# Starting layer 2's masked weights inside layer 1's last group, with a shrinking lead

## The chip, the cores and the metric

The kernel runs on one core of one Trainium2 chip. The metric is the device time of one execution in microseconds (us). The engines are TensorE (PE, matrix products), VectorE (DVE, elementwise), ScalarE (ACT, activations), GpSimd (POOL) and SyncE (SP, which issues most DMAs). Each engine works its own queue in order and waits on semaphores for the others.

## The reference, cut to what matters

Four layers of graph attention work on x (16 batches, 1024 nodes, 64 channels, float32) and one adjacency matrix adj (1024 x 1024). After each, x becomes layernorm(x + layer(x)). Layer 1 and layer 2 are the ones around the change:

```python
# layer 1: softmax over the neighbours, for each channel by itself
feat = softplus(x * (INV_SQRT2 * w0) + b0)
scores = feat * wa + ba
attn = softmax(where(mask, scores, -1e9), over neighbours)      # mask = adj > 0
out = einsum('bijd,bjd->bid', attn, feat)

# layer 2 (layer 0 is of the same form)
h = input @ W
e = (h @ a1)[:, :, None] + (h @ a2)[:, None, :]
e = where(e > 0, e, 0.2 * e)
attention = softmax(where(adj > 0, e, -9e15))
out = elu(attention @ h)
```

Layer 3 has four heads of dot-product attention and an output layer of the same kind.

## The kernel before, in words

The 1024 nodes are 8 chunks (C) of 128, and the 16 batches (B) are 4 groups (NG) of 4 (GB) in layer 1.

**Layer 1** is a sum over neighbours of numerator and denominator, each split in a high and a low part (`hi`, `lo`). `product_l1(g, ic)` is 16 products on PE for chunk `ic` of group `g` (L1966). `average(g, ic)` takes the logarithm and the exponential on ACT (L1976, L1977), four passes on DVE (L1979 to L1984) and four `bn_stats` (L1986). Results lie in a PSUM pool with two buffers. Between the chunks stand hand-placed tasks: `ahead` (preparations for the next group, in the last group those of layer 2) and `last` (the previous group's or layer's endings: `root`, `shift` and eight `rows` tasks, which scale eight rows each on ACT, L780). A scheduler orders the engines' queues here.

**Layer 2** is `gat_layer` with `zero_mean`. Its engines' queues keep the written order. For batch b and chunk k:

- `unit(k)` on DVE (L1026) makes the masked weights of 128 x 1024, e = max(G, q) * aT. G is the exponential of the scores for a pair of batches, q a factor per node, aT the mask. The `e` tiles have 7 buffers in this layer.
- `product(k, e)` on PE (L1038) multiplies them with `vals`, four matmul instructions of 64 x 512 in the trace (two calls).
- The loop `go()` runs over t = 0 to 15 and k = 0 to 7. In each step it issues unit k, queues the product of the unit two steps before (LAG = 2), and then the tasks that `slots[(t, k)]` holds.
- The ends of a batch are among these: `evict` (ACT, L1057), `project` (PE, L1070), `divide` (DVE reciprocal and ACT `l_sums`, L1114), `quotients` (ACT L1124 and the exponential m, L1136), `residual` (DVE v and m, L1141, L1142), `norm` (DVE), `root`, `shift`, `store` (ACT, L780).
- So are the preparations for a pair of batches: `prep_x` (transposes, PE L933, ACT L934), `prep_s` (scores, PE L940), `prep_top` (DVE maximum L951, ACT copy `l_s` L952, POOL all-reduce L957), `prep_p` (four small ACT instructions, L965 to L974), `prep_G` for two halves (PE `pg` L987, ACT exponential into G, L996, from a PSUM pool with one buffer), and `prep_v` (ACT, nine small instructions into `vals`, L1006, L1008).

Before the change, batch 0's x, scores, top and p are in the last group of layer 1, and its G and vals are written after that group. The first unit follows layer 1's last average and moments. Layer 1's last four batches get their rows (`last`) within the first steps of layer 2.

```python
e = unit(k)
behind(lambda product=product, k=k, e=e: product(k, e), LAG if zero_mean else 2 * LAG)
```

Of the kernel before, what the change touches and what calls it, by code (L numbers as in the profile page):

```python
# [8 lines left out]
F32 = mybir.dt.float32  # L9
F32R = mybir.dt.float32r  # L10
# [6 lines left out]
P = 128  # L17
# [20 lines left out]
LAG = 2  # L38
# [544 lines left out]
def fast_path(  # L583
# [25 lines left out]
    B, N, D = x.shape  # L609
    C = N // P  # L610
# [4 lines left out]
    NG = B // GB  # L615
    HALF = N // 2
    CH = C // 2
# [4 lines left out]
    ep = ctx.enter_context(tc.tile_pool(name="ep", bufs=2))  # L622
# [6 lines left out]
    for g in range(NG):  # L629
        t = xpool.tile([P, C, GB, D], F32, tag=f"x{g}", name=f"x{g}")  # L630
# [161 lines left out]
    def behind(step, lag):  # L792
        waiting.append(step)
        while len(waiting) > lag:
            waiting.pop(0)()
# [6 lines left out]
    aT = const.tile([P, C, N], BF16, tag="aT", name="aT")  # L802
# [108 lines left out]
    def gat_layer(w, name, zero_mean, own, room=None):  # L911
# [3 lines left out]

        w1, w4, ind, s12, sums, w_out = (w[k] for k in ("w1", "w4", "ind", "s12", "sums", "out"))
        F = D - 1 if zero_mean else D
        xT, G, pgs, pq, vals, only, stats = {}, {}, {}, {}, {}, {}, {}
        if not zero_mean:
            ring = [gp.tile([P, C, 32], F32, tag=f"only{r}", name=f"only{r}", bufs=1) for r in range(4)]  # L920
            for t in ring:
# [65 lines left out]
                nc.tensor.matmul(parts[i], w1[rows, :], xT[b][h][rows, :], start=True, stop=True)  # L987

        def exps_G(b, h):
            if h == 0:  # L990
                G[b] = gp.tile([P, 2, N], F32, tag="G", name=f"G_{name}_{b}")
            cols = slice(h * HALF, (h + 1) * HALF)
            parts = pgs[b, h]
            for i, part in enumerate(parts):
                dst = G[b][:, :, cols] if len(parts) == 1 else G[b][:, i, cols]
                nc.scalar.activation(dst, part, AF.Exp, bias=pq[b][2], scale=1.0 - ALPHA)  # L996

        def prep_G(b, h):
            scores_G(b, h)
# [1 line left out]

        def prep_v(b):
            p = pq[b - b % 2][0][:, :, b % 2]
            v = gp.tile([P, C, D], F32, tag="vals", name=f"vals_{name}_{b}", bufs=3)
            for c in range(C):
                nc.scalar.activation(v[:, c, :F], xb(b)[:, c, :F], AF.Copy, scale=p[:, c : c + 1])  # L1006
            if zero_mean:
                nc.scalar.copy(v[:, :, F], p)  # L1008
            else:
                only[b] = ring[b % 4]  # L1010
                nc.scalar.copy(only[b][:, :, b % 2], p)
            vals[b] = v

        def attention(b):
# [7 lines left out]
            begins, closes = b % 2 == 0 or not joint, b % 2 == 1 or not joint  # L1022

            def unit(k):
                e = gp.tile([P, N], F32, tag="e", name="e", bufs=7 if zero_mean else 10)
                nc.vector.scalar_tensor_tensor(  # L1026
                    e, G[b - b % 2][:, b % 2, :], pq[b - b % 2][1][:, k, b % 2 : b % 2 + 1], aT[:, k, :],
                    ALU.max, ALU.mult,
                )
                return e  # L1030
# [149 lines left out]
        def at(t, k, task):  # L1180
            slots.setdefault((t, k), []).append(task)

        work = [attention(b) for b in range(B)]
        if zero_mean:
            ends = [(1, 1), (1, 3), (1, 4), (1, 5), (2, 0), (2, 1)]
# [7 lines left out]
        for b in range(B):  # L1193
            places = ends[b % 2]
# [11 lines left out]
        ahead = []  # L1206
        for b in range(0, B, 2):
            halves = (range(CH), range(CH, C)) if zero_mean else (range(C), ())
            chain = [
                lambda b=b: prep_x(b, 0), lambda b=b: prep_x(b, 1), *(lambda b=b, c=c: prep_s(b, c) for c in halves),  # L1210
                lambda b=b: prep_top(b), lambda b=b: prep_p(b), lambda b=b: prep_G(b, 0),
                lambda b=b: prep_G(b, 1), lambda b=b: prep_v(b), lambda b=b: prep_v(b + 1),
            ]
            if zero_mean:
                places = (-2, 0), (-2, 1), (-2, 5), (-2, 6), (-1, 0), (-1, 2), (-1, 3), (-1, 4), (-1, 2), (0, 4)
            else:
                places = (-3, 3), (-3, 3), (-3, 7), (-3, 7), (-2, 1), (-2, 3), (-2, 7), (-1, 3), (-1, 4), (0, 4)
            if b == 0 and not zero_mean:
                chain[6:8] = [lambda f=f, h=h: f(0, h) for f in (scores_G, exps_G) for h in range(2)]
                ahead = chain[:-1]  # L1220
                at(0, 4, chain[-1])
                continue
            if b == 2 and not zero_mean:
                places = (-2, 4), (-2, 5), (-2, 6), (-2, 6), (-2, 6), (-2, 7), (-1, 1), *places[7:]
            for task, (t, k) in zip(chain, places):
                if b + t >= 0:
                    at(b + t, k, task)
                elif b:
                    at(0, 0, task)
                else:  # L1230
                    ahead.append(task)
        if room:
            ahead[-3:-1] = [lambda f=f, h=h: f(0, h) for f in (scores_G, exps_G) for h in range(2)]

        def go(extra, opening=()):
            for (t, k), todo in extra.items():
                for task in todo:
                    at(t, k, task)
            with tc.manual_schedule(engines=in_order):
                for task in opening:  # L1240
                    task()
                for t in range(B + 1):
                    for k in range(C):
                        catch_up()
                        if t < B:
                            unit, product, _ = work[t]
                            e = unit(k)
                            behind(lambda product=product, k=k, e=e: product(k, e), LAG if zero_mean else 2 * LAG)
                        elif t == B and k == 0:
                            drain()  # L1250
                        if t < B or (t == B and k < own):
                            for task in slots.get((t, k), []):
                                task()

            return [
                task for t in range(B, B + 3) for k in range(C) for task in slots.get((t, k), []) if (t, k) >= (B, own)
            ]
# [567 lines left out]
    def prep_l1(g, q):  # L1825
# [36 lines left out]

        def back():
            if q == 0:
                his[g] = l1["halves"].tile([P, C, 2, 2, P], F32R, tag="hi", name=f"hi{g}")
                los[g] = l1["halves"].tile([P, C, 2, 2, P], F32R, tag="lo", name=f"lo{g}")
            t = h["t"]
            pe = l1["psum"]("pe")
            for c in range(C):
                nc.tensor.transpose(pe[:, c, :], t[:, c, :], ident)  # L1870
            hi, lo = his[g][:, :, q, 1, :], los[g][:, :, q, 1, :]
            nc.scalar.copy(hi, pe)
            nc.vector.tensor_tensor(h["f"], h["f"], pe, ALU.mult)
            nc.vector.tensor_tensor(lo, pe, hi.bitcast(F32), ALU.subtract)
# [11 lines left out]
    with tc.tile_pool(name="ps_g", bufs=1, space=bass.MemoryType.PSUM, reuse_waits="tile") as ps_g, tc.tile_pool(  # L1886
# [64 lines left out]
    l2_ahead, l2_go = gat_layer(later["w2"], "l2", True, 2, room=dict(  # L1951
        xT=lambda: [ep.tile([P, C, D], F32, tag="v", name="xT").rearrange("p c d -> p (c d)") for _ in range(2)],
        g=lambda: l1["psum"]("pg").rearrange("p (i c) q -> p i (c q)", i=2),
    ))
    l1_psum = ExitStack()
    ps_l = l1_psum.enter_context(tc.tile_pool(name="ps_l", bufs=2, space=bass.MemoryType.PSUM, reuse_waits="tile"))
    with tc.tile_pool(name="l1", bufs=2, reuse_waits="tile") as pool:
# [36 lines left out]
        for g in range(NG):  # L1994
            ahead = [[] for _ in range(C)]
            for q in range(2 if g + 1 < NG else 0):

                for ic, task in zip((q, q, q, q, q + 1, q + 2, q + 2, q + 4, q + 5), prep_l1(g + 1, q)):
                    ahead[ic].append(task)
            if g + 1 == NG:  # L2000
                for ic, task in zip((1, 2, 3, 3, 4, 5, 6, 6), l2_ahead):
                    ahead[ic].append(task)
            st = pool.tile([P, C * GB, 6], F32, tag="st1", name=f"st{g}")
            for ic in range(C):
                po = product_l1(g, ic)
                average(g, ic, po, st)
                for task in ahead[ic] + last[ic : ic + 1]:
                    task()
            y = xg[g].rearrange("p c b d -> p (c b) d")
            mo = {}  # L2010

            root, finish = moments(st)

            def shift(mo=mo, end=finish):
                mo["n"] = end()

            def rows(c, y=y, mo=mo):
                scaled(y, y, mo["n"], range(c * 8, c * 8 + 8))

            last = [root, shift] + [lambda c=c, rows=rows: rows(c) for c in range(C * GB // 8)]  # L2020
    l1_pools.close()

    l3a = ctx.enter_context(tc.tile_pool(name="l3a", bufs=2, side="right", reuse_waits="tile"))

# [73 lines left out]

    gat = ExitStack()
    gp = gat.enter_context(tc.tile_pool(name="gat2", bufs=2, reuse_waits="tile"))
    for task in l2_ahead[8:]:
        task()
    l1_psum.close()
    with tc.tile_pool(name="ps_g", bufs=1, space=bass.MemoryType.PSUM, reuse_waits="tile") as ps_g, tc.tile_pool(
        name="ps_p", bufs=1, space=bass.MemoryType.PSUM, reuse_waits="tile"
# [9 lines left out]
                nc.vector.tensor_tensor(own, own, ident16, ALU.max)  # L2117

        extra.setdefault((B, 1), []).append(own_nodes)
        ending = l2_go(extra)  # L2120
    gat.close()
    for j, task in enumerate(ending):
        at(0, j, task)

# [121 lines left out]
```

## Time and profile before

| | |
|---|---|
| time, median of 3 runs | 1936.0 us (1935.41 to 1936.15) |
| profiled execution | 1936.93 us, its span 1935.0 us |
| mean granted PE clock | 0.987 of full speed |
| busy in the span | PE 1869.8, DVE 1754.3, ACT 1324.6, POOL 78.7 us |
| span of layer 0 | 0 to about 285 us |
| span of layer 1 | about 280 to 421 us |
| span of layer 2 | about 421 to 630 us |
| span of layer 3 | about 630 to 1935 us |

Busy times are those of one profiled execution. Matrix products overlap in the pipeline, so a busy PE isn't at its peak. A line of a timeline gives start, duration, engine, source line, operation, output <- inputs, the count of like instructions run together, and in brackets the idle time just before it and what ended it. The granted clock is a share of full speed.

### The profile page before, as it was taken

What the parts mean: (1) busy time and instruction counts of PE and PEld (TensorE: products, weight loads), DVE (VectorE), ACT (ScalarE), POOL (GpSimd) and SP (SyncE); (2) the same over time, 40 slices, a digit from 0 to 9 for tenths busy, and PEclk for the clock granted to TensorE, in tenths of its full rate; (3) what the DMA queues carried; (4) which work ended last, traced back from release to release, by engine and by line L of the source; (5) the groups of instructions that cost most, each with busy time, mean ns of one, the idle gap of its engine ahead of it and who ended that gap; (6) DMA issues with size and microseconds to landing.
All of it is one profiled execution on the core that took longest, in us unless ns stands there. A gap on an engine that the chain in (4) does not pass through costs nothing. (4 is left out here: it accounts for less than half of the span.)

```text
span 1935.0 us, 25703 instructions
## 1 busy us (share of the span) xinstructions
PE 1869.8 (97%) x9505; PEld 764.4 (40%) x9505; DVE 1754.3 (91%) x2924; ACT 1324.6 (68%) x2350; POOL 78.7 (4%) x77
## 2 busy tenths in 40 slices
PE   8999989989998999999999999999999999999996
PEld 4334347864333333333333333333333333333332
DVE  6999988879999879799998998989989899899996
ACT  4556567857778776676767766777676776776754
POOL 0000000000000000000000000000000000000001
PEclk9999989999999999999999999999999999999998
DMA  7000000000000110000000000010000100000000
GB/s 182 1 1 1 1 1 1 1 1 1 1 1 12 54 46 12 12 23 18 12 17 18 23 18 12 18 28 12 18 12 18 29 12 18 12 27 20 12 23 13
DMA packets 45746, 35.87 MB, mean 19 GB/s; under 512 B 37295, under 2 KB 37616, under 8 KB 45614
## 3 DMA queue, kind: packets, MB, share of 16 engines
q1 hardware_dynamic: 43534, 33.64, 6.7%
q8 instruction: 76, 1.25, 0.3%
q10 hardware_dynamic: 2080, 0.52, 0.1%
q14 instruction: 56, 0.46, 0.1%
HBM read 29.45 MB, written 4.70 MB: 18 GB/s over the span
## 5 line engine op out<-in xcount | busy, mean ns | idle before, releaser
L1413 ACT ACTIVATE e<-s,shift 128x1024 f32<-128x1024 f32 x512 | 538.5, 1122 | 240.1 <-PE s L1409 240.1
L1417 DVE TENSOR_TENSOR e<-e,aT 128x1024 f32<-128x1024 f32 x512 | 596.1, 1215 | 4.8 <-ACT e L1413 4.8
L1409 PE MATMUL s<-hT 64*128 64x512 f32 x2048 | 489.2, 602 | 2.5 <-ACT zT L1456 1.4
L1424 PE MATMUL y<-e,vals 128*64 128x512 f32 x2048 | 483.4, 599 | 2.2 <-DVE e L1417 1.3
L1026 DVE SCALAR_TENSOR_TENSOR e<-G_l,q,aT 128x1024 f32<-128x1024 f32 x256 | 314.8, 1275 | 0.9 <-ACT G_l L996 0.7
L1409 PEld LDWEIGHTS s<-hT 64*128 64x128 f32 x2048 | 183.6, 185 | 287.9 <-issue 142.2
L1038 PE MATMUL y_l<-e,vals_l 128*64 128x512 f32 x1024 | 253.8, 618 | 19.9 <-DVE e L1026 13.4
L1424 PEld LDWEIGHTS y<-e,vals 128*64 128x64 f32 x2048 | 135.2, 136 | 269.3 <-issue 199.7
L1593 DVE TENSOR_TENSOR e<-e,aT 128x1024 f32<-128x1024 f32 x128 | 156.4, 1225 | 13.1 <-ACT e L1580 3.1
L1585 DVE SCALAR_TENSOR_TENSOR junk<-e,aN 128x1024 bf16<-128x1024 f32 x120 | 146.1, 1217 | 0.0
L1580 ACT ACTIVATE e<-s,shift 128x1024 f32<-128x1024 f32 x128 | 138.6, 1113 | 3.9 <-PE s L1575 3.9
L1575 PE MATMUL s<-h2T 64*128 64x512 f32 x512 | 127.4, 598 | 0.0
L1601 PE MATMUL y<-e,h2v 128*64 128x512 f32 x512 | 125.6, 592 | 0.0
L1038 PEld LDWEIGHTS y_l<-e,vals_l 128*64 128x64 f32 x1024 | 63.3, 138 | 152.1 <-issue 85.7
L1966 PE MATMUL po<-hi,aR 128*128 128x512 f32 x256 | 103.8, 406 | 11.1 <-ACT hi L1878 7.3
L1352 POOL PARTITION_ALL_REDUCE gtop<-top x48 | 54.9, 1144 | 1253.6 <-DVE top L1350 928.7
L1966 PE MATMUL po<-lo,aR 128*128 128x512 f32 x256 | 102.2, 400 | 0.0
L780 ACT ACTIVATE x<-m,bn_shift,bn_rstd 128x64 f32<-128x64 f32 x224 | 77.4, 429 | 13.0 <-DVE bn_shift L771 13.0
L1575 PEld LDWEIGHTS s<-h2T 64*128 64x128 f32 x512 | 51.8, 189 | 60.0 <-issue 39.0
L1456 ACT COPY zT<-poT 64x512 f32<-64x512 f32 x124 | 72.0, 581 | 1.1
L1431 ACT COPY yT<-y 128x512 f32<-128x512 f32 x64 | 38.4, 600 | 43.9 <-PE y L1424 42.9
L1601 PEld LDWEIGHTS y<-e,h2v 128*64 128x64 f32 x512 | 36.6, 137 | 73.6 <-issue 59.9
(283 smaller groups left out, 1880.3 us busy)
## 6 DMA issues: line engine op xcount, KB each, us to landing
r<-inverse SPq DMA_DIRECT2D x62, 256.0 KB
adj<-in_adj_dram SPq DMA_DIRECT2D x16, 512.0 KB
out_dram<-res SPq DMA_DIRECT2D x15, 256.0 KB
x<-in_x_dram SPq DMA_DIRECT2D x14, 256.0 KB
rows<-yT SPq DMA_DIRECT2D x62, 4.0 KB
x<-in_x_dram ACTq DMA_DIRECT2D x2, 256.0 KB
sums<-rows SPq DMA_DIRECT2D x31, 8.0 KB
inverse<-rt SPq DMA_DIRECT2D x31, 8.0 KB
```

The costliest lines, as they stand in the source:

```text
L1026: nc.vector.scalar_tensor_tensor(e, G[b - b % 2][:, b % 2, :], pq[b - b % 2][1][:, k, b % 2 : b % 2 + 1], aT[:, k, :], ALU.max, ALU.mult,)
L1038: nc.tensor.matmul(held["y"][h * D : (h + 1) * D, :], vals[b][:, k, :], e[:, h * HALF : (h + 1) * HALF], start=(k == 0), stop=(k == C - 1),)
L1409: nc.tensor.matmul(s[:, i, :], hT[rows, k * P : (k + 1) * P], hT[rows, cols], start=True, stop=True)
L1413: nc.scalar.activation(e, s, AF.Exp, bias=shifts[b, n])
L1417: nc.vector.tensor_tensor(e, e, bc_mid(aT[:, k, h * HALF : (h + 1) * HALF], 2), ALU.mult)
L1424: nc.tensor.matmul(held[h][i * D : (i + 1) * D, :], vals[b][:, k, :], e[:, i, :], start=(k == 0), stop=(k == C - 1),)
L1575: nc.tensor.matmul(s[:, i, :], hT[rows, (i + k // CH) % 2, k % CH * P : (k % CH + 1) * P], hT[rows, 0, :], start=True, stop=True,)
L1580: nc.scalar.activation(e, s, AF.Exp, bias=shifts[b])
L1585: nc.vector.scalar_tensor_tensor(junk.rearrange("p c q -> p (c q)").bitcast(BF16), e.rearrange("p i q -> p (i q)"), 1.0, aN[:, k, :], ALU. ...
L1593: nc.vector.tensor_tensor(e, e, aT[:, k, :].rearrange("p (i q) -> p i q", i=2), ALU.mult)
L1601: nc.tensor.matmul(held["o"][h * D : (h + 1) * D, :], vals["out", b][:, k, :], e[:, h, :], start=(k == 0), stop=(k == C - 1),)
L1966: nc.tensor.matmul(po.rearrange("p q k f -> p (q k f)"), aR[:, k, ic * P : (ic + 1) * P], e[:, k].rearrange("p q k f -> p (q k f)"), start ...
```

## The change

It adds no arithmetic. It does these things:

- The eight units of batch 0 are issued in layer 1's last group, one after chunk 1, 2, 3, 4, 5 and 6 and two after chunk 7 (`made` keeps the tiles). G of batch 0 and its vals are now written at the start of that group (its tasks stand after chunk 0 and chunk 1), and x, scores, top and p of batch 0 in the group before it (after chunks 4 to 7). In the last group DVE's written order is kept.
- The `e` tiles have ten buffers in this layer, two of their own and eight in the tiles that hold `hi` and `lo` of the even groups of layer 1 (the odd groups keep theirs in another pool). G and vals of batch 0 use buffers of other tags, for which layer 1's pools are closed only in step (5, 0) of layer 2.
- In layer 2, step n issues units up to n + lead(n), where lead is 7 and shrinks by one every 14 units. In the first batch a product is queued in its own step, not two later.
- The preparations of the pairs from batch 2 on are placed earlier by the lead, all but `prep_v`.
- In every group of layer 1, a chunk's `last` task comes before its `ahead` tasks.

```diff
         def exps_G(b, h):
+            apart = room and b == 0
             if h == 0:
-                G[b] = gp.tile([P, 2, N], F32, tag="G", name=f"G_{name}_{b}")
+                G[b] = room["G"]() if apart else gp.tile([P, 2, N], F32, tag="G", name=f"G_{name}_{b}")
...
             def unit(k):
-                e = gp.tile([P, N], F32, tag="e", name="e", bufs=7 if zero_mean else 10)
+                n = (b * C + k) % 10
+                if room and n < C:
+                    e = room["e"](n)
+                else:
+                    e = gp.tile([P, N], F32, tag="e", name="e", bufs=2 if room else 10)
...
+        def lead(n):
+            return max(0, 7 - n // 14) if room else 0
...
+            if room and b:
+                n = lead((b - 1) * C)
+                sooner = [divmod((b + t) * C + k - n, C) for t, k in places[:8]]
+                if b == 2:
+                    begin, chain = chain[:2], chain[2:]
+                    sooner = [(0, k) for k in range(1, 7)]
+                places = [(t - b, k) for t, k in sooner] + list(places[8:])
...
         if room:
             ahead[-3:-1] = [lambda f=f, h=h: f(0, h) for f in (scores_G, exps_G) for h in range(2)]
+            ahead += [room["begin"], *(lambda k=k: made.update({k: work[0][0](k)}) for k in range(C))]
...
-                            unit, product, _ = work[t]
-                            e = unit(k)
-                            behind(lambda product=product, k=k, e=e: product(k, e), LAG if zero_mean else 2 * LAG)
+                            n = t * C + k
+                            for u in range(n, min(n + lead(n), B * C - 1) + 1):
+                                unit_ready(u)
+                            product, e = work[t][1], made.pop(n)
+                            lag = 2 * LAG if not zero_mean else LAG if t else 0
+                            behind(lambda product=product, k=k, e=e: product(k, e), lag)
...
-                his[g] = l1["halves"].tile([P, C, 2, 2, P], F32R, tag="hi", name=f"hi{g}")
-                los[g] = l1["halves"].tile([P, C, 2, 2, P], F32R, tag="lo", name=f"lo{g}")
+                home = l1["halves"] if g % 2 else l1["both"]
+                his[g] = home.tile([P, C, 2, 2, P], F32R, tag="hi", name=f"hi{g}", bufs=1)
+                los[g] = home.tile([P, C, 2, 2, P], F32R, tag="lo", name=f"lo{g}", bufs=1)
...
-            if g + 1 == NG:
-                for ic, task in zip((1, 2, 3, 3, 4, 5, 6, 6), l2_ahead):
-                    ahead[ic].append(task)
+            places = {NG - 2: (4, 4, 5, 5, 6, 7), NG - 1: (0, 0, 0, 1, 1, 1, 1, 2, 3, 4, 5, 6, 7, 7)}.get(g, ())
+            for ic, task in zip(places, l2_ahead[6 if g + 1 == NG else 0 :]):
+                ahead[ic].append(task)
...
-            for ic in range(C):
-                po = product_l1(g, ic)
-                average(g, ic, po, st)
-                for task in ahead[ic] + last[ic : ic + 1]:
-                    task()
+            with ExitStack() as order:
+                if g + 1 == NG:
+                    order.enter_context(tc.manual_schedule(engines={mybir.EngineType.DVE}))
+                for ic in range(C):
+                    po = product_l1(g, ic)
+                    average(g, ic, po, st)
+                    for task in last[ic : ic + 1] + ahead[ic]:
+                        task()
...
-    for task in l2_ahead[8:]:
-        task()
...
+        extra.setdefault((5, 0), []).append(open_l3a)
```

More of the change, by code (lines that the diff above doesn't have):

```diff
@@ L917, in gat_layer @@
         F = D - 1 if zero_mean else D
-        xT, G, pgs, pq, vals, only, stats = {}, {}, {}, {}, {}, {}, {}
+        xT, G, pgs, pq, vals, only, stats, made = {}, {}, {}, {}, {}, {}, {}, {}
         if not zero_mean:
@@ L989, in exps_G, with of_pair @@
         def exps_G(b, h):
+            apart = room and b == 0
             if h == 0:
-                G[b] = gp.tile([P, 2, N], F32, tag="G", name=f"G_{name}_{b}")
+                G[b] = room["G"]() if apart else gp.tile([P, 2, N], F32, tag="G", name=f"G_{name}_{b}")
             cols = slice(h * HALF, (h + 1) * HALF)
-            parts = pgs[b, h]
+            parts = [pgs[b, h][0][:, i, :] for i in range(2)] if apart else pgs[b, h]
             for i, part in enumerate(parts):
-                dst = G[b][:, :, cols] if len(parts) == 1 else G[b][:, i, cols]
+                dst = G[b][:, :, cols] if len(parts) == 1 else of_pair(b, i)[:, cols]
                 nc.scalar.activation(dst, part, AF.Exp, bias=pq[b][2], scale=1.0 - ALPHA)
+        def of_pair(b, i):
+            return G[b][i] if isinstance(G[b], list) else G[b][:, i, :]
         def prep_G(b, h):
@@ L1003, in prep_v @@
             p = pq[b - b % 2][0][:, :, b % 2]
-            v = gp.tile([P, C, D], F32, tag="vals", name=f"vals_{name}_{b}", bufs=3)
+            if room and b == 0:
+                v = room["vals"]()
+            else:
+                v = gp.tile([P, C, D], F32, tag="vals", name=f"vals_{name}_{b}", bufs=3)
             for c in range(C):
@@ L1024, in unit @@
             def unit(k):
-                e = gp.tile([P, N], F32, tag="e", name="e", bufs=7 if zero_mean else 10)
+                n = (b * C + k) % 10
+                if room and n < C:
+                    e = room["e"](n)
+                else:
+                    e = gp.tile([P, N], F32, tag="e", name="e", bufs=2 if room else 10)
                 nc.vector.scalar_tensor_tensor(
-                    e, G[b - b % 2][:, b % 2, :], pq[b - b % 2][1][:, k, b % 2 : b % 2 + 1], aT[:, k, :],
+                    e, of_pair(b - b % 2, b % 2), pq[b - b % 2][1][:, k, b % 2 : b % 2 + 1], aT[:, k, :],
                     ALU.max, ALU.mult,
@@ L1233, in gat_layer, with unit_ready @@
             ahead[-3:-1] = [lambda f=f, h=h: f(0, h) for f in (scores_G, exps_G) for h in range(2)]
+            ahead += [room["begin"], *(lambda k=k: made.update({k: work[0][0](k)}) for k in range(C))]
+        def unit_ready(u):
+            if u not in made:
+                made[u] = work[u // C][0](u % C)
         def go(extra, opening=()):
@@ L1239, in go @@
             with tc.manual_schedule(engines=in_order):
-                for task in opening:
+                for task in begin if room else opening:
                     task()
@@ L1953, in fast_path @@
         g=lambda: l1["psum"]("pg").rearrange("p (i c) q -> p i (c q)", i=2),
-    ))
+        G=lambda: [l1["pool"].tile([P, C, P], F32, tag="t", name=f"G{i}").rearrange("p c q -> p (c q)") for i in range(2)],
+        vals=lambda: ep.tile([P, C, D], F32, tag="m", name="vals", bufs=4),
+        begin=lambda: l1.update(
+            e=[l1["both"].tile([P, CH, N], F32, tag=t, name=f"e_{t}", bufs=1) for t in ("hi", "lo")]
+        ),
+        e=lambda k: l1["e"][k // CH][:, k % CH, :],
+    ))
+    both = ExitStack()
+    l1["both"] = both.enter_context(tc.tile_pool(name="both", bufs=1, reuse_waits="tile"))
     l1_psum = ExitStack()
@@ L2020, in fast_path, with open_l3a @@
             last = [root, shift] + [lambda c=c, rows=rows: rows(c) for c in range(C * GB // 8)]
-    l1_pools.close()
-    l3a = ctx.enter_context(tc.tile_pool(name="l3a", bufs=2, side="right", reuse_waits="tile"))
+    l3a = None
+    def open_l3a():
+        nonlocal l3a
+        l1_pools.close()
+        l3a = ctx.enter_context(tc.tile_pool(name="l3a", bufs=2, side="right", reuse_waits="tile"))
     slots, mids = {}, {}
@@ L2119, in fast_path @@
         extra.setdefault((B, 1), []).append(own_nodes)
+        extra.setdefault((5, 0), []).append(open_l3a)
         ending = l2_go(extra)
     gat.close()
+    both.close()
     for j, task in enumerate(ending):
```

## The prediction

> **What bounds the kernel now.** I read the page's busy shares first, then the windows around the end of layer 1, the VectorE (DVE) timeline across it, the TensorE (PE) and ScalarE (ACT) timelines behind it, and the groups of layer 2. Windows: busy time of PE, weight loads, DVE, ACT and POOL, then the granted clock.
> ```profile
> 385.00:400.00 15.00, 15.00 (x73) 12.01 (x73) 11.15 (x45) 5.92 (x21) 0.35 (x1) 1.00 0.00 1
> 400.00:421.00 21.00, 21.00 (x92) 16.55 (x91) 13.69 (x48) 12.45 (x38) 0.00 (x0) 1.00 0.00 1
> ...
> 422.50:427.40 4.90, 0.01 (x1) 0.00 (x0) 4.62 (x17) 4.87 (x16) 0.00 (x0) 0.86 0.00 2
> 427.40:432.90 5.50, 5.43 (x14) 1.76 (x16) 5.40 (x9) 2.44 (x10) 0.00 (x0) 0.50 0.00 1
> ...
> 460.00:480.00 20.00, 18.70 (x90) 6.62 (x86) 19.93 (x36) 18.22 (x57) 1.24 (x1) 1.00 0.00 1
> ```
> The last group of layer 1 (about 394 to 421) is bound by PE, which is never idle; DVE has a third of it free. Layer 2 (about 426 to 629) is bound by DVE, 19.93 of 20 us. Between them lies the seam: PE stands from 422.5 to 427.4, and then runs 5.5 us at a granted clock of 0.50.
>
> DVE's timeline shows both halves: the free third (idle before each average, released by ACT) and what layer 2 begins with.
> ```profile
> 410.55 0.42 DVE L1979 TENSOR_TENSOR t<-po,r 128x256 f32<-128x256 f32 x1 [1.12 <-ACT r L1977]
> ...
> 413.98 0.42 DVE L1979 TENSOR_TENSOR t<-po,r 128x256 f32<-128x256 f32 x1 [0.99 <-ACT r L1977]
> ...
> 417.60 0.42 DVE L1979 TENSOR_TENSOR t<-po,r 128x256 f32<-128x256 f32 x1 [1.18 <-ACT r L1977]
> ...
> 422.54 0.42 DVE L1979 TENSOR_TENSOR t<-po,r 128x256 f32<-128x256 f32 x1 [2.50 <-PE pxT L933]
> ...
> 429.21 8.46 DVE L1026 SCALAR_TENSOR_TENSOR e<-G_l,q,aT 128x1024 f32<-128x1024 f32 x7
> ...
> 446.89 1.28 DVE L1026 SCALAR_TENSOR_TENSOR e<-G_l,q,aT 128x1024 f32<-128x1024 f32 x1 [0.70 <-ACT G_l L996]
> 449.19 0.69 DVE L1141 SCALAR_TENSOR_TENSOR v<-v,x 128x512 f32<-128x512 f32 x1 [1.01 <-ACT m L1136]
> ```
> Seven units take 8.46, so a unit costs 1.21. After 449.2 DVE has no gap over 0.7 until layer 2 ends: a stall or gain of DVE here goes whole into the time, and layer 3 behind it only shifts. PE's timeline at the seam:
> ```profile
> 421.48 1.04 PE L933 MATMUL pxT<-ident,x 128*128 128x128 f32 x8
> 427.46 6.32 PE L1038 MATMUL y_l<-e,vals_l 128*64 128x512 f32 x16 [4.95 <-ACT bn_rstd L708]
> ...
> 443.29 1.08 PE L1038 MATMUL y_l<-e,vals_l 128*64 128x512 f32 x4
> 444.57 1.13 PE L987 MATMUL pg<-xT_l,l_w 64*128 64x512 f32 x4 [0.21 <-ACT l_sums L1114]
> 445.63 3.65 PE L1038 MATMUL y_l<-e,vals_l 128*64 128x512 f32 x16
> ```
> Four units' products (x16) take 3.65 at full clock, 0.9 a unit, and 6.32 at half clock, about 1.7 a unit with the ramp. A half of the scores of G (pg) is 1.1, by the same ratio 2.1 at half clock.
>
> **The change, part by part.** No arithmetic is added or removed; instructions change place. Times below are in before's clock.
>
> 1. *Batch 0's units in the last group: -6.15.* An average costs DVE 2.47 a chunk, PE's 16 products 3.62; with a unit DVE needs 3.67. Six units (0 to 5) lie in these gaps, 6 x 1.21 = 7.25. DVE becomes longer than PE by 0.05 a chunk and starts each average where the unit ends, so average 7 starts at 423.7 in place of 422.54: 1.1 is given back. Units 6 and 7 come after it, on the path as before. PE waits at most 0.3 for its double buffer, inside that 1.1. Were the gaps closed, all 7.25 would be back.
>
> 2. *Batch 0's preparations.* Its x, scores, top and p move to group 2, its G and vals to the boundary: PE still has to do 2 x 1.06 of pg, ACT 2 x 1.1 of G. PE's end stays at 421.45, since it only exchanges places inside a stage that PE fills; ACT has 8.5 of 21 us free there. At nothing; without that cover, about 4 us. POOL's all-reduce of batch 0 (1.24) and SP's row stores keep their order.
>
> 3. *`last` ahead of `ahead` in every group: +0.7.* In group 0 the exp of the last batch of layer 0 (m, 0.63 on ACT) and two residuals (0.69 each on DVE) now go before the casts `hi` and `lo` that PE waits for at 280.0 (it idles 7.3 us there). Bounds: 0, if these casts end last elsewhere, and 2.0 (0.63 + 1.38) if they add. I take 0.7, the ACT part, nearest to the row that releases PE. All other groups have their casts a whole group early.
>
> 4. *Lead of seven with ten buffers.* Before, the ring had seven buffers and no lead: PE could lag seven steps before DVE waited. Now unit n+10 needs product n finished, and with the units issued seven ahead PE may lag three steps (3.6 us). Waits come from PE's written order: pg's second half (one PSUM buffer) waits for the exps of the first, and products queue behind it on PE.
>    - Pair 1 (batches 2, 3): PE starts product 0 at 422.5 with no idle, does p0 to p5, the scores, pg half 0 and p6 (5.3 + 2.0 + 1.1 + 0.9) by about 431.8, and stands at pg half 1. That waits for: average 7 to 426.2, moments 1.0, u6 and u7 2.4, Newton step 0.8, u8 to u10 3.6, top 0.2 (434.3); ACT l_s 0.2, vals 2.2, p and q 0.65, G half 0 1.05 (438.35). PE idles 6.6, more than the 4.95 which in the row above halved the clock. pg half 1 then takes 2.1, G 1.05: u16 at 441.5, where DVE stands since 440.4: +1.1. Before, the same place waited 0.70, and v 1.01 for ACT: -1.7 for both.
>    - Behind it at half clock: u20 waits for p10 (447.7) +1.1, v for m +0.55, small ones +0.55 (0.40 at the Newton step, 0.15 at G).
>    - Pair 2 (batches 4, 5): after top at 456.25 ACT has in order l_s 0.2, eight rows of layer 1's last group 2.65, sums 0.15, vals 2.2, p 0.65, quotients 1.75, m 0.55, G half 0 1.05: 465.2. p21 stands behind pg half 1, and u31 needs p21: at half clock 465.2 + 2.1 + 1.7, u31 waits 3.4; at full clock 1.55. PE's idle before it is 4.65. The reciprocal behind it: 0.75 at half clock.
>    - From batch 6 the lead is five and falling, one more step of slack every 14 units, while PE needs about 10.5 us a batch and DVE 12.0: PE catches up and I find no wait longer than a few tenths.
>
>    Sum of waits: with half clock after both idles 0.55 + 1.1 + 1.1 + 0.55 + 3.4 + 0.75 = 7.45; after the first alone 0.55 + 1.1 + 1.1 + 0.55 + 1.55 = 4.85; in neither 2.6 (u16, u20 and the reciprocal pay nothing). The second idle (4.65) is just under the 4.95 that is shown to halve it, so I take the middle, 6.15.
>
> The clock row matters most here. A much shorter idle halved it as well in this trace: PE stood 1.81 us at 317.3 and the clock was 0.51 from 320.4 to 323.7.
> ```profile
> 319.15 0.47 PE L1966 MATMUL po<-hi,aR 128*128 128x512 f32 x1 [1.81 <-DVE top L1858]
> ```
> ```profile
> 320.40:323.70 3.30, 3.30 (x9) 2.52 (x9) 3.13 (x16) 1.20 (x1) 0.00 (x0) 0.51 0.00 0
> ```
> [...]
>
> **Sum:** -6.15 - 1.7 + 6.15 + 0.7 = -1.0 against the profiled execution's 1936.93 (span 1935.0 and 1.9 around it): 1935.9. That execution lies 0.9 above the median of the runs, 1936.0, so 1935.0. A measurement of this kernel can tell about 0.2%, 3.9 us, from no change. Its own range, with part 3 from 0 to 2.0 and the waits from 4.85 to 7.45: 1933 to 1938.
>
> **Rivals.**
> A. *The waits stay small.* If PE's clock comes back at once, or idles are shorter than drawn, waits are 2.6: -6.15 - 1.7 + 2.6 + 0.7 = -4.55, 1931.5; with none at all 1929. For it: PE starts 5 us earlier and has 1.5 us a batch in hand. Against it: the 5.5 us at 0.50 behind 4.9 of idle.
> B. *Slower: the chain top, ACT, pg half 1, product, unit closes into a ring.* With ten buffers and a lead of five to six, the pairs 3 and 4 pay 3.4 each as pair 2 does: 7.45 + 6.8 gives +7.1, 1943.1. It decides once PE's lag at each second pg exceeds four steps (4.8 us). For it: ACT is busy 18.22 of 20 us, its eight rows of 2.7 lie in that chain every batch there, and a step of slack returns only every 14 units. Against it: PE catches up 1.5 a batch.
> C. *The units don't fit.* If a unit beside PE and ACT costs more than the gap, all averages lag, PE's double buffer stalls and part 1 gives half, about 3: with the other terms +2, 1938.
>
> **Chances.** Forecast 0.37, A 0.31, B 0.24, C 0.08. Below 1932.1: most of A and the lower edge of the forecast, 0.33. Above 1939.9: B and tails of C and the forecast, 0.28. Rest 0.39. Range: from A's 1929.5 to short of B's far end, 1942.
>
> **What would show it.** Right: average 7 starts near 424.4 (423.7 and the 0.7), product 0 near 423.2 without idle, two PE idles of 4 to 7 us near 435 and 461 with a clock near 0.5 behind, DVE waits on G and on products of 1 to 3.5 up to batch 4, none behind. Wrong: DVE waits at batches 6 to 9 (B), PE idles without a clock drop (A), PE waiting for DVE in the last group (C), a start of group 0 moved by more than 1 us or not at all (part 3).

## The result and the profile after

Over 20 runs of each kernel the median is 1937.95 us (1935.3 to 1940.16) after and 1935.22 us (1931.94 to 1938.63) before; the ratio is 1.0016, with a 95% interval of 1.0009 to 1.0023. The kernel is slower by about 2.7 us. That lies inside the stated range and inside 0.2%, but on the other side of zero from the forecast of -1.0.

The two profiled executions hide this: their spans are 1935.1 after and 1935.0 before. They have to be cut by stage. Layer 1, from PE's first product to its last, took 139.34 after and 141.61 before; layer 2, from there to layer 3's first masked tile, 213.87 and 210.02; the rest 1301.48 and 1303.31. Layer 1's difference is mostly the clock. PE stands 1.81 us in the same place in both, and in only one of the two executions the granted clock fell behind it. The window of layer 1 from 315 to 330, before and then after (busy PE, weight loads, DVE, ACT, POOL, then the clock):

```profile
315.00:330.00 15.00, 13.19 (x56) 10.63 (x55) 12.35 (x48) 7.63 (x16) 0.00 (x0) 0.89 0.00 1
```
```profile
315.00:330.00 15.00, 13.19 (x63) 10.83 (x62) 13.60 (x51) 9.24 (x22) 0.00 (x0) 1.00 0.00 1
```

The change itself is in layer 2. First its good half, in the windows after: PE is still full in layer 1's last group, and DVE's busy time there is 23.45 of 27.00 (17.99 before). Then the two places where PE stands and the stretches behind them.

```profile
394.00:421.00 27.00, 27.00 (x124) 22.09 (x124) 23.45 (x66) 17.38 (x52) 0.00 (x0) 1.00 0.00 1
429.00:435.50 6.50, 1.25 (x6) 0.20 (x4) 6.50 (x8) 3.82 (x15) 1.24 (x1) 0.92 0.00 1
435.50:437.50 2.00, 1.99 (x4) 0.50 (x4) 2.00 (x2) 0.00 (x0) 0.00 (x0) 0.50 0.00 0
458.00:462.80 4.80, 0.68 (x4) 0.00 (x0) 4.12 (x5) 4.74 (x19) 0.00 (x0) 0.89 0.00 0
462.80:464.80 2.00, 1.97 (x4) 0.51 (x4) 0.42 (x1) 0.00 (x0) 0.00 (x0) 0.50 0.00 0
```

PE's timeline has the reason: it stands in its own queue before pg's second half, which waits for ACT, and runs it and the products behind it at about half speed (2.08 for what takes 1.13 in the first half at 456.54).

```profile
420.54 1.94 PE L1049 MATMUL y_l<-e_hi,vals 128*64 128x512 f32 x8
...
435.51 2.08 PE L987 MATMUL pg<-xT_l,l_w 64*128 64x512 f32 x4 [5.26 <-ACT G_l L997]
...
456.54 1.13 PE L987 MATMUL pg<-xT_l,l_w 64*128 64x512 f32 x4
...
462.83 2.08 PE L987 MATMUL pg<-xT_l,l_w 64*128 64x512 f32 x4 [4.15 <-ACT G_l L997]
464.83 4.62 PE L1049 MATMUL y_l<-e_hi,vals_l 128*64 128x512 f32 x12
```

DVE's timeline has what that costs, the waits in the brackets. Written u16 is unit 16, the first of batch 2, and p10 the product of unit 10; unit n + 10 takes the buffer of unit n and so waits for product n (the ring). The lines with brackets are u16, u19, u20, v, u31, a reciprocal, and v twice.

```profile
438.78 2.48 DVE L1037 SCALAR_TENSOR_TENSOR e_lo<-G_l,q,aT 128x1024 f32<-128x1024 f32 x2 [1.20 <-ACT G_l L997]
...
442.88 1.28 DVE L1037 SCALAR_TENSOR_TENSOR e<-G_l,q,aT 128x1024 f32<-128x1024 f32 x1 [0.35 <-PE y_l L1049]
...
445.42 3.67 DVE L1037 SCALAR_TENSOR_TENSOR e_hi<-G_l,q,aT 128x1024 f32<-128x1024 f32 x3 [1.13 <-PE y_l L1049]
...
461.81 0.69 DVE L1152 SCALAR_TENSOR_TENSOR v<-v,x 128x512 f32<-128x512 f32 x1 [0.65 <-ACT m L1147]
...
466.85 1.29 DVE L1037 SCALAR_TENSOR_TENSOR e_hi<-G_l,q,aT 128x1024 f32<-128x1024 f32 x1 [3.63 <-PE y_l L1049]
...
472.30 0.21 DVE L1125 RECIPROCAL rt<-po 128x8 f32<-128x8 f32 x1 [0.76 <-PE po L1081]
...
509.45 0.20 DVE L1125 RECIPROCAL rt<-po 128x8 f32<-128x8 f32 x1
...
514.16 0.69 DVE L1152 SCALAR_TENSOR_TENSOR v<-v,x 128x512 f32<-128x512 f32 x1 [0.89 <-ACT m L1147]
...
537.98 0.69 DVE L1152 SCALAR_TENSOR_TENSOR v<-v,x 128x512 f32<-128x512 f32 x1 [0.89 <-ACT m L1147]
```

With 0.33 at the Newton step and 0.18 at a reciprocal at 496.7 that makes 10.0 us of waits up to unit 112, the first of batch 14, where before had 1.7. Unit 112 begins 178.6 us after PE's last product of layer 1, against 176.4 before: 2.2 later. So the early units brought 10.0 - 1.7 - 2.2 = 6.1 us, and the waits took 8.3. With 0.4 to 0.9 at the start of layer 1 (a layer 1 longer by 0.42, and up to 0.52 ahead of its first product, below) that is 2.6 to 3.1, and the medians differ by 2.7.

Two falls of the clock are not counted in this. At layer 2's end the after execution loses another 1.6 at a fall (0.67 from 614.5 to 619.6) behind an idle of 2.15 us that ends at 614.5; the before execution also has that idle, without the fall (1.00 from 612 to 622). From 610 to 622 the granted clock was below 1 in e1_lead0 (0.89), e2_lead4 (0.86) and e7_lead0_late (0.96) too, and 1.00 in e3_act, e6_ring11 and e9_act2. Near layer 3's end it is the other way round: before has a fall (0.62 and 0.52 in the two stretches of 2 us from 1896.7 to 1900.7) and after has none there (1.00 from 1890 to 1910), which is about the 1.8 by which its rest is shorter. Whether that is chance was not tested. With both counted the sum is 2.4 to 2.9.

### The profile page after: what moved, and what is told of

The parts are those of the page before. It is cut to its first block, busy times and chain, and to the rows that moved or that the text cites. A ratio compares the mean times of both kernels' runs of the same rounds, so it can differ in the third digit from the quotient of the medians.

```text
span 1935.1 us, 25705 instructions
## 1 busy us (share of the span) xinstructions
PE 1868.5 (97%) x9505; PEld 765.4 (40%) x9505; DVE 1754.7 (91%) x2924; ACT 1324.9 (68%) x2352; POOL 78.9 (4%) x77
## 5 line engine op out<-in xcount | busy, mean ns | idle before, releaser
L1037 DVE SCALAR_TENSOR_TENSOR e<-G_l,q,aT 128x1024 f32<-128x1024 f32 x150 | 186.0, 1277 | 0.6 <-PE y_l L1049 0.4
L1049 PE MATMUL y_l<-e,vals_l 128*64 128x512 f32 x608 | 147.1, 609 | 3.5 <-DVE e L1037 3.4
L1049 PEld LDWEIGHTS y_l<-e,vals_l 128*64 128x64 f32 x608 | 38.5, 137 | 78.7 <-issue 61.3
```

What stands on the lines that cost most here:

```text
L1037: nc.vector.scalar_tensor_tensor(e, of_pair(b - b % 2, b % 2), pq[b - b % 2][1][:, k, b % 2 : b % 2 + 1], aT[:, k, :], ALU.max, ALU.mult,)
L1049: nc.tensor.matmul(held["y"][h * D : (h + 1) * D, :], vals[b][:, k, :], e[:, h * HALF : (h + 1) * HALF], start=(k == 0), stop=(k == C - 1),)
```

## The experiments

All change the changed kernel and were timed against the kernel before. "At unit 112" is that unit's start after PE's last product of layer 1, less the 176.4 of before, from one profiled execution; the waits are those of DVE up to that unit, each of 0.15 us and more.

| run | ratio to before, 95% | at unit 112 | DVE's waits |
|---|---|---|---|
| the change | 1.0016 (1.0009 to 1.0023) | +2.2 | 10.0 |
| e1_lead0 | 0.9987 (0.9978 to 0.9995) | -5.3 | 3.3 |
| e2_lead4 | 1.0000 (0.9991 to 1.0008) | -2.2 | 6.2 |
| e3_act | 1.0040 (1.0026 to 1.0053) | +7.2 | 14.6 |
| e4_warm | 1.0022 (1.0013 to 1.0031) | +4.3 | 12.3 |
| e5_warm2 | 0.9995 (0.9986 to 1.0004) | -2.3 | 6.0 |
| e6_ring11 | 1.0003 (0.9994 to 1.0012) | +0.9 | 8.7 |
| e7_lead0_late | 0.9975 (0.9965 to 0.9985) | -7.3 | 1.1 |
| e8_lead0_late_order | 0.9969 (0.9957 to 0.9980) | -5.8 | 2.7 |
| e9_act2 | 1.0021 (1.0011 to 1.0030) | +7.7 | 15.4 |

The two columns differ by up to some 3.6 us: e1_lead0 is 5.3 ahead at unit 112 and 2.5 by its ratio, e9_act2 7.7 behind and 4.1 by its ratio. "At unit 112" is one execution, and it leaves out what stands ahead of PE's last product of layer 1 and behind that unit. So gains are taken from the ratios, and the places of the waits from the profiles.

### Is it the lead or the early units? (e1_lead0, e2_lead4)

```diff
-            return max(0, 7 - n // 14) if room else 0
+            return 0                                      # e1_lead0
+            return max(0, 4 - n // 14) if room else 0     # e2_lead4
```

> The changed kernel with lead(n) = 0: batch 0's eight units stay in layer 1's last group, but no later unit is issued ahead of its step and no preparation is moved by a lead. Theory (the lead of seven with ten buffers is what loses the time; the head start of 6.1 us is sound): PE no longer stands 5.3 and 4.2 us at the second half of pg, DVE's waits in layer 2 fall from 10.0 us in the changed kernel to about 3, and the time is 4 to 5 us under the kernel before (ratio 0.9975). Rival (without the lead each batch's ends, the reciprocal and v first, come to DVE before PE has the products): DVE waits there for 8 us or more and the time stays at 1.0016 or above.

> The changed kernel with a lead of 4 that shrinks by one every 14 units in place of 7. Theory: three more steps of slack in the ring and preparations three units earlier in DVE's order, so the waits for G and for products mostly go and 2 to 4 us remain: ratio 0.998 to 0.999. Rival (the lead is needed to keep the ends of batch 0 off DVE's path): waits move to the reciprocal and v, no gain, 1.0015.

Without a lead the kernel is faster than before, by 0.13%. PE's idles before pg's second half are 1.82 and 0.21 in place of 5.26 and 4.15, since `top` stands three units earlier in DVE's order and starts ACT's chain sooner. Apart from 0.33 at the Newton step, one wait is left, the first batch's reciprocal, as the rival had it, but of 2.92 and not 8. The gain is 2.5 us and not the 4 to 5 of the theory. DVE with lead 0:

```profile
437.23 0.21 DVE L1125 RECIPROCAL rt<-po 128x8 f32<-128x8 f32 x1 [2.92 <-PE po L1081]
```

A lead of four lies between the two (1.0000): no waits for e buffers, but 3.72 at a reciprocal behind an idle PE of 3.69, and waits of about 1 and less. The theory's 0.998 to 0.999 was too good. The intervals of lead 0 and of the change do not overlap: the early units are sound, and the lead, with the places of the preparations that follow it, is what loses the time. Which of these two does it was not tried apart.

### Is it the clock behind PE's idles? (e4_warm, e5_warm2)

```diff
         def prep_G(b, h):
+            if room and h == 1 and b in (2, 4):
+                junk = ps_t.tile([P, HALF], F32, tag="t", name="junk")
+                for _ in range(2 * (6 - b // 2)):         # e5_warm2: range(6 - b // 2)
+                    nc.tensor.matmul(junk, w1[:D, :], xT[b][h][:D, :], start=True, stop=True)
             scores_G(b, h)
```

> The changed kernel with extra products without use on PE before the second half of pg of batches 2 and 4 (10 and 8 matmul calls of 64 x 512, about 5.3 and 4.2 us at full clock), in the places where PE stands idle. They leave the results as they are. Theory (half of the waits are the clock that falls behind PE's idle): PE stays at full clock, pg half 1 takes 1.1 in place of 2.1, u16 waits 0.2 in place of 1.2, the two waits after it go, u31 waits about 1.6 in place of 3.6; the time falls by 3 to 5 us against the changed kernel (0.999 of before). Rival (the clock doesn't matter, ACT's chain sets all of it): within 1 us of the changed kernel, 1.0015.

The first of them failed by its size: a call took 0.89 us and not 0.53, so the 10 and 8 calls ran for 8.9 and 7.1 us, longer than the idles, and pg came later than in the changed kernel (waits of 3.51 and 6.08 at u16 and u31). It says nothing on the clock. The second has half as many.

> As the run with extra products, but 5 and 4 calls in place of 10 and 8, by the 0.886 us that a call took there (8.42 us for 19 instructions of 0.44): 4.4 and 3.5 us, inside PE's idles of 5.26 and 4.15. Theory (behind PE's idles it is the halved clock that costs): pg half 1 takes 1.1, u16 waits 0.2 in place of 1.2, the waits of 0.35 and 1.13 behind it go, u31 waits about 1.7 in place of 3.6, the reciprocal 0: 4 to 5 us less than the changed kernel, 0.999 to 0.9995 of before. Rival (the clock doesn't matter): 1.0015.

Its PE timeline and windows: the work without use fills both idles, pg's second half takes 1.13, and the clock stays at 1.00.

```profile
429.01 4.56 PE L1006 MATMUL junk<-xT_l,l_w 64*128 64x512 f32 x10
...
434.32 1.13 PE L987 MATMUL pg<-xT_l,l_w 64*128 64x512 f32 x4 [0.76 <-ACT G_l L997]
...
454.69 3.70 PE L1006 MATMUL junk<-xT_l,l_w 64*128 64x512 f32 x8
...
458.92 1.13 PE L987 MATMUL pg<-xT_l,l_w 64*128 64x512 f32 x4 [0.53 <-ACT G_l L997]
```
```profile
434.30:436.50 2.20, 2.18 (x10) 0.79 (x12) 2.08 (x2) 1.00 (x1) 0.00 (x0) 1.00 0.00 0
...
459.00:461.00 2.00, 2.00 (x10) 0.67 (x12) 0.31 (x1) 0.91 (x1) 0.00 (x0) 1.00 0.00 0
```
```profile
436.64 2.48 DVE L1041 SCALAR_TENSOR_TENSOR e_lo<-G_l,q,aT 128x1024 f32<-128x1024 f32 x2 [0.26 <-ACT G_l L997]
...
461.10 1.28 DVE L1041 SCALAR_TENSOR_TENSOR e_hi<-G_l,q,aT 128x1024 f32<-128x1024 f32 x1 [1.79 <-PE y_l L1053]
```

u16's wait is 0.26 (1.20), u31's 1.79 (3.63), and the two waits between are gone, all as expected. The time fell by 0.0021 of 1935, 4.1 us; unit 112 is 4.5 us earlier. So the halved clock made about half of the 8.3 us. Work that computes nothing made the kernel faster than the change, though not measurably faster than before.

### Is it the ring? (e6_ring11)

```diff
-                n = (b * C + k) % 10
+                n = (b * C + k) % 11
...
-                    e = gp.tile([P, N], F32, tag="e", name="e", bufs=2 if room else 10)
+                    e = gp.tile([P, N], F32, tag="e", name="e", bufs=3 if room else 10)
```

> The changed kernel with one more buffer for e, eleven. Lead and orders stay. Theory (a lead of seven leaves three steps in a ring of ten): u31 then needs product 20, which stands ahead of pg half 1 on PE, so its 3.6 goes; what remains is u32's wait for G itself, about 2 to 3, and u20's waits of 1.5 fall by about 1.2. In all 2 to 3 us less than the changed kernel, 1.000 of before. Rival (ACT's chain to G alone sets it, and the ring is no cause): u31's wait turns up whole at u32, within 1 us of the changed kernel, 1.0015.

u20's 1.13 and u31's 3.63 are gone, and so is the reciprocal's 0.76 behind them; in their place stand 1.31 for a product at u32 and 1.95 and 0.94 at reciprocals, the last one behind a stretch from 477.5 in which PE, with no idle before it, takes 1.64 and 1.93 for four products each in place of 1.08 (see the end). So of 5.5 us about 4.2 comes back as other waits, since PE is late all the same. The ratio 1.0003 says 2.5 us less than the change, with intervals that overlap a little, unit 112 says 1.3. The ring is a cause, the smaller one, and its size is not settled.

### Is it ACT's order? (e3_act, e9_act2)

```diff
+            if room and b <= 2:
+                places = *places[:-1], (0, 7)
...
-        for p, task in zip(((0, 0), (0, 1), (2, 2), (2, 6), (3, 7), (4, 2)), last):
+        for p, task in zip(((0, 0), (0, 1), (6, 2), (6, 6), (7, 7), (8, 2)), last):    # e3_act
+        for p, task in zip(((0, 0), (0, 1), (2, 7), (2, 7), (3, 7), (4, 2)), last):    # e9_act2
```

> The changed kernel with ACT work moved out of the chain that releases pg's second half: the eight small vals instructions of batches 1 and 3 go three steps later, and the four rows tasks of layer 1's last group four batches later. Lead, ring and PE order stay. Theory (the chain top, ACT, pg half 1, product, unit is what waits): the chain is 2.2 us shorter for batch 2 and 4.9 us shorter for batch 4, PE's idles fall to about 3 and under 1, u16's wait of 1.2 and u31's of 3.6 go, and the time is 3 to 4 us under the kernel before (0.998). Rival (the ring of ten with lead seven is too short by itself): waits of the same size at other units, 1.0015.

> The changed kernel with the ACT chain to pg's second half shortened as in the third experiment, but with the rows tasks kept in batch 2: the vals instructions of batches 1 and 3 stand three steps later, and the rows of step (2, 2) stand in (2, 7), behind G of that pair. Theory (the chain of ACT work ahead of pg half 1 makes PE's idles; in the third experiment it was the rows in batches 6 and 7 that lost the time): the trace is that of the third experiment up to unit 56, 3.3 us ahead of the changed kernel, and this time the lead is kept: 3 us less than the changed kernel, 1.000 of before. Rival (a shorter chain only moves the waits on): within 1 us of the changed kernel, 1.0015.

Both missed. In e3_act PE's second idle fell to 1.93 and u31 waited 1.06, and unit 56 was 3.3 us ahead of the changed kernel; then the moved rows stood in the same chain of batches 6 to 9, PE's idle at 514 grew from 1.23 to 3.88, DVE waited 2.95 at a reciprocal and 3.79 for the scores of a later pair, and more was lost than gained. In e9_act2 sixteen rows in one piece on ACT (5.42 us) stood before the copy yT, and a reciprocal waited for it:

```profile
465.64 5.42 ACT L780 ACTIVATE x<-x,bn_shift,bn_rstd 128x64 f32<-128x64 f32 x16
470.95 0.57 ACT L1068 COPY yT_l<-y_l 128x512 f32<-128x512 f32 x1
```
```profile
473.72 0.21 DVE L1125 RECIPROCAL rt<-po 128x8 f32<-128x8 f32 x1 [5.38 <-PE po L1081]
```

The later vals kept PE waiting too (1.30 and 0.48 on L1015). The rival is right for the time: moving ACT work between the first batches moves the wait. That ACT's chain sets the length of the first idles is shown all the same, by e3_act up to unit 56 and by the same idles of e9_act2 (4.58 and 1.93, 4.57 and 1.94, in place of 5.26 and 4.15).

### A version that beats both (e7_lead0_late, e8_lead0_late_order)

```diff
+            return 0
...
+            if room and b == 0:
+                places = [*places[:2], (1, 6), (1, 7), (2, 2), (2, 3), (2, 3), (2, 3), places[-1]]
...
-                    for task in last[ic : ic + 1] + ahead[ic]:
+                    for task in last[ic : ic + 1] + ahead[ic] if g + 1 == NG else ahead[ic] + last[ic : ic + 1]:    # e8
```

> Lead 0 as in the first experiment, with batch 0's reciprocal, quotients, residual and norm two to five steps later in the written order. Theory (lead 0 leaves one wait, 2.92 at batch 0's reciprocal, since DVE reaches it before PE has the batch): that wait goes, 2.5 to 3 us less than with lead 0, 0.9972 of before. Rival (the wait only moves to the next batch's reciprocal or to v): within 1 us of lead 0, 0.9987.

> As the run before it, and in groups 0 to 2 of layer 1 a chunk's ahead tasks come before its last task again. Theory (the new order delays the casts that PE waits for at the start of group 0 by 0.5 to 0.8 us): ACT's cast hi and DVE's lo of the second half come without m, v and m between, PE's first product is 3.2 us after the start of the cast of the mask in place of 3.7, and the time is 0.5 to 0.8 lower than in the run before it. Rival (nothing there is on the path): no difference at PE's start.

With the first reciprocal two steps later its wait is 0.52 in place of 2.92, unit 112 is 7.3 us ahead of before, and the ratio, 0.9975, says 4.8. It is 2.3 us under lead 0 by the ratios, near the 2.5 to 3 expected, but their intervals overlap; the waits fell by 2.2.

e8_lead0_late_order shows the cost of the new order at layer 1's start. From the start of ACT's last cast of the mask to PE's first product it is 3.18 us with the old order and 3.70 with the new one; layer 1 took 138.89 against 139.31. ACT in the changed kernel, with m between the two casts, and then in this run:

```profile
276.70 1.05 ACT L2030 CAST aR<-aT 128x1024 fp32r<-128x1024 bf16 x1
277.65 0.64 ACT L1147 ACTIVATE m<-v 128x512 f32<-128x512 f32 x1
...
279.31 1.03 ACT L1909 CAST hi<-f 128x1024 fp32r<-128x1024 f32 x1
```
```profile
278.90 1.05 ACT L2032 CAST aR<-aT 128x1024 fp32r<-128x1024 bf16 x1
...
280.99 1.04 ACT L1911 CAST hi<-f 128x1024 fp32r<-128x1024 f32 x1
```

Its ratio, 0.9969, is the best of all, 6 us under before, but its interval overlaps that of the run without the order; only the rows tell these two apart. (Its unit 112 is later than that run's: this execution had a fall of the clock that is shown at the end, with waits of 0.81 and 1.01 behind it.)

## Why the prediction failed

- **The head start, -6.15: right in kind, and its size partly by luck.** It is 6.1 by the balance above, but the same balance gives 6.9 in e1_lead0 (5.34 + 3.25 - 1.71) and 6.7 in e7_lead0_late. Average 7 began 1.44 after PE's end, which is 0.4 later than before (1.06), where 1.1 was drawn: 7.25 - 0.4 is 6.85. What is missing of it in the changed kernel fits waits under 0.15 us, which the list leaves out. PE did not wait in the last group.
- **Batch 0's preparations at nothing: right.** PE is 26.00 of 26.00 from 395 to 421 in both.
- **The order in group 0, +0.7: about right.** The first product is 0.52 later against the cast, the first lo product another 0.27.
- **The places and sizes of the waits: right one by one.** Drawn and measured: PE's idles 6.6 and 4.65, 5.26 and 4.15; u16 1.1, 1.20; the wait for p10 1.1, 0.35 and 1.13; v 0.55, 0.65; u31 3.4, 3.63; the reciprocal 0.75, 0.76. With the small ones the list with both falls of the clock, 7.45, measured 8.05.
- **The sum that was taken from the list, 6.15: a step that failed.** It is the middle between one fall of the clock and two, taken because the second idle (4.65) was just under the 4.95 that had shown a fall. Both idles (5.26 and 4.15) were followed by 0.50, so the list with both falls was the one to take. The row of 1.81 us in the same text had already shown 0.51 behind a much shorter idle. This is 1.3 of the error, and 0.6 more is the early waits that were drawn too small (8.05 for 7.45).
- **"No wait longer than a few tenths" from batch 6 on: the larger step that failed, a term put at nothing.** v waits 0.89 for m twice and a reciprocal waits 0.18, 1.96 us in all. The shrinking of the lead itself makes the two longer ones: in a step where the lead falls no unit is issued, and two of these steps (56 and 70) lie between a batch's reciprocal and its v. So only three units, 3.82 us with what stands among them, lie between the reciprocals at 509.45 and 533.27 and v, while ACT takes 4.68 from the reciprocal to the end of m. Before has four units there (4.86 from the reciprocal at 506.33 to v), ACT takes 4.69, and nothing waits:

```profile
506.45 4.83 DVE L1026 SCALAR_TENSOR_TENSOR e<-G_l,q,aT 128x1024 f32<-128x1024 f32 x4
```

The prediction counted the shrinking as slack alone. e5_warm2 and e6_ring11 keep both waits (0.90), so they come neither from the clock nor from the ring; e1_lead0 has neither. 1.3 + 0.6 + 1.96 is the 3.85 by which the waits exceed the forecast: -1.0 became +2.7 or so.
- **Two readings.** DVE does have a gap over 0.7 behind 449.2, 0.95 at the reciprocal at 627.91. And a gain of DVE did not go whole into the time: with lead 0 the 5.3 at unit 112 were 3.7 at layer 2's end, with a granted clock of 0.89 between 610 and 622, and 2.5 by the ratio.
- **The clock behind an idle: no middle was shown.** Layer 2's PE timelines show ten idles of PE from 2.96 to 5.26 us, and behind all ten PE's groups soon took about twice their usual time: pg's second half 2.08 (after, behind 5.26 and 4.15; e3_act 4.58; e9_act2 4.57; e2_lead4 3.69; e6_ring11 5.25) and 1.97 (e6_ring11 2.96) in place of 1.13; eight of `po` 2.10 in place of 1.16 (e9_act2 3.84); sixteen products 6.32 in place of 3.65 (before, 4.95); and, behind a pg of 1.13, eight products 3.58 in place of 1.94 (e3_act 3.88). The granted clock was 0.50 there before and after, and in e9_act2 from 436 to 442. The idles of 1.81 us at 317 and of 2.15 us at 614 were followed by a fall in one of the two executions before and after and not in the other. So the runs give no ground for the middle at the second idle (drawn 4.65, measured 4.15).
- **The rivals.** A (small waits) is refuted for this kernel; e5_warm2, with the clock at 1.00 in both places, still waits 6.0 us. B had the sign and the mechanism for pair 2, but pairs 3 and 4 did not pay 3.4 each; PE's idles there are 2.23 and 1.23, and DVE waits 0.89 at most. C did not occur.

## What to carry to other kernels

Work moved early into another stage's gaps is kept only if what follows it in each queue has its slack still; here the buffers and the written order of PE's work gave back more than the gaps brought, and the plain version without the lead was the better one. A lead that shrinks leaves steps without a unit, and here the ACT work that had run beside that unit was then waited for. In a kernel like this one a drawn idle of PE of 3 us or more should be priced with the halved clock behind it (here PE ran at about half speed behind all ten of 2.96 to 5.26 us), not at an average of the cases. And two single executions with equal spans can differ by stage: cut the span at the stages before saying that nothing moved.

## What the runs showed of the hardware that was not expected

- In layer 1's stretch from 315 to 330, which holds the idle of 1.81 us (317.3 to 319.1 before), the granted clock was 0.89 before and in e4_warm and 1.00 in the other nine profiles. This scatter (0.11 of 15 us, about 1.7) is about as large as the effects studied here, and it shifts whole layers between two executions.
- The five falls between 300 and 640 us in the two profiles before and after lasted, by the granted clock, 3.4 us (before from 320.3, after from 615.3) and 6.8 us (before from 426.0, after from 434.4 and from 461.7).
- The clock also fell with PE never idle: in e8_lead0_late_order it is 0.50 from 454 to 456, right behind the second of two groups of eight small matmuls (128x4, 1.05 us a group) among full products; the twelve products behind it take 4.49 in place of 2.79. The same stands in e4_warm (twelve in 4.49 from 456.45, 0.50 from 457 to 459), and PE slows down in the same place in e5_warm2 (eight products in 3.59 from 474.1, in place of 1.94), e6_ring11 (from 477.5) and e9_act2 (eight in 3.38 from 484.0). Other passes of the same groups had none (after at 450.86, twelve products in 2.79). Why was not tried.

```profile
452.00:454.00 2.00, 2.00 (x10) 1.07 (x11) 1.97 (x3) 2.00 (x6) 0.00 (x0) 0.66 0.00 0
454.00:456.00 2.00, 2.00 (x6) 0.48 (x4) 2.00 (x9) 1.25 (x5) 1.24 (x1) 0.50 0.00 0
```
